# The last key block in 64-row tiles, with its values kept twice beside zeros, and the loading of gated weights alternated with bias additions

## Chip, cores and metric

The kernel runs on one core of a Trainium2 chip. The metric is the device time of one execution in microseconds, and the figure for a kernel is the median of its runs. The engines are named as the profile names them: PE multiplies matrices (PEld is its loading of weights), DVE, ACT and POOL work on elements, and SP issues most of the transfers.

## What is computed

One transformer block on x of 2 x 1024 x 256 with a context of 2 x 154 x 192, all in float32: self-attention, attention to the context, and a gated feed-forward layer, each behind a LayerNorm and with a residual. There are 16 heads of 64.

```python
def _attention(xq, xkv, wq, wk, wv, wo, bo):
    ...
    attn = jnp.einsum('bihd,bjhd->bhij', q, k) * scale
    attn = jax.nn.softmax(attn, axis=-1)
    out = jnp.einsum('bhij,bjhd->bihd', attn, v).reshape(B, S, D_ATTN)
    return out @ wo + bo
h = _layernorm(x, ln1_g, ln1_b)
x = _attention(h, h, sa_wq, sa_wk, sa_wv, sa_wo, sa_bo) + x
h = _layernorm(x, ln2_g, ln2_b)
x = _attention(h, cond_emb, ca_wq, ca_wk, ca_wv, ca_wo, ca_bo) + x
h = _layernorm(x, ln3_g, ln3_b)
p = h @ ff_w1 + ff_b1
a, gate = (p[..., :D_FF], p[..., D_FF:])
h = a * jax.nn.gelu(gate, approximate=False) @ ff_w2 + ff_b2
return h + x
```

## The kernel before

**Three loops of slots.** All work is issued in an order written out by hand. A first loop of 128 slots (`p`) does self-attention, a second of 48 slots (`c`) does the attention to the context, and a third (`k`, counted on as `c = 48 + k` by the helpers of the second) does the feed-forward layer. A unit is one pair of heads of one batch, so there are 16 units in each attention. A unit of self-attention takes eight slots, one of the second attention three (groups of 3, 3 and 2 row tiles of 128 queries). Beside its own work a slot takes pieces from lists: `work` (projections of the next unit), `side` (pieces of a LayerNorm), `outs` (output projections of units that are done), `stores` and `adds` (copies out of PSUM and additions to x, run a little later), and `later` (transfers and bias additions; two entries a slot in the second loop, one in the others).

**A unit of the second attention.** `cross_first(c)` computes scores into two PSUM banks (L654), DVE takes the negated maximum (`neg`, L659), ACT the exponents with their sums (L670), DVE the reciprocals (`rden`, L678), POOL scales (L681). Two slots on, `cross_turn` transposes 32x32 blocks on DVE into a ring of three units (`pT_ca`, L697). The context's 154 keys are padded with zeros to 160, five blocks of 32. `cross_regroup` moves the first four blocks of the ring by transfers (L714, on SP) into `pairs`, a part of the tile `wf`, so that pairs of blocks lie in 64 rows. The fifth block stays in the ring: its rows 32 x a4 to 32 x a4 + 31 hold the keys 128 to 159 for the quarter a4 of the queries.

**Weighing.** `cross_values(ui, a2)` does two of the four quarters, a2 and 2 + a2, seven slots after the unit's first slot for a2 = 0 and eight for a2 = 1. For m = 0 and 1 it takes 64-row tiles from `pairs`; for m = 2 it takes 32-row tiles from the ring. Every float32 matmul of the program appears as two in the profile, so a weighing is 16 matmuls of 64x64 tiles (`poc<-wf,v_ca`) and 8 of 32x64 (`poc<-pT_ca,v_ca`), all on L730. Its sums are copied out by DVE (`o_ca`, L743).

**The values.** `values()` projects values once for two units (L618), in the last slot before the even unit begins: in slot p = 125 of the first loop for unit 0, then at c = 5, 11, 17, 23, 29, 35 and 41. In the next slot ACT copies them (L627, and L628 for the fifth block, 32 rows). Entries put at the head of `later` copy by transfers: L630 mirrors the first blocks into the other 64 rows, and L635 repeats the 32 rows of the fifth block at rows 32, 64 and 96. The tile has the tag `V`, with two buffers that the self-attention's values also use.

**PSUM.** Projections, keys (L606), values and the LayerNorm transposes (`ph_ln`, L227, copied out by ACT on L240) share two banks in turn (`mm_tile`). In the first slot of a unit two q projections stand one behind the other (L299, copied on L308), so the second needs a bank that something else has freed.

**LayerNorms beside.** While the second attention runs, the LN2 of the second batch (slots 9 to 17) and the LN3 of the first batch (around slots 39 to 46) are done in pieces: statistics (L196, L197) and offset (`off_ln`, L212) on DVE, variance and power on POOL (L202, L206), normalizing on ACT (`xn_ln`, L218), transposes on PE, and L240.

**The gated layer's weights.** At c = 5 `hold_gated()` takes a buffer for `wf` and appends 12 transfers of 256 KB to `later`: 8 for w1 (L794) and 4 for w2 (L797). `add_biases("ca", 0)` appends 8 additions of the bias to x on POOL (L261) behind them. Since the copies of values go to the head of the list and take slots 6, 12 and 18, the transfers run in slots 5 and 7 to 11, the additions in 13 to 16.

**Self-attention, as far as it matters here.** A slot p computes two groups of scores (L382), DVE reduces them (L542), ACT takes exponents (L393). Partial maxima and sums are exchanged between rows by transfers (`st<-st`, L403); the slot after joins them (`dd` L411 to L413 on POOL, `ee` L415 on ACT, `zz` and `den` L417 and L419 on POOL, `rd` L489 on DVE) and scales on POOL (L493). DVE transposes the groups of two slots ago (L507), and `weigh` multiplies with the values (`po`, L429, 64x64 tiles).

Of the kernel before, what the change touches and what calls it, by code (L numbers as in the profile page):

```python
# [8 lines left out]
F32 = mybir.dt.float32  # L9
# [4 lines left out]
P = 128  # L14
# [4 lines left out]
def tile_transformer_block(ctx: ExitStack, tc: tile.TileContext, a: dict, out: bass.AP):  # L19
    nc = tc.nc  # L20
# [6 lines left out]
    DF = w["ff_w2"].shape[0]  # L27
    DH = 64
# [5 lines left out]
    NC = D // P  # L34
    CC = DC // 2
    KP = T // 2
    KB = 32
    NB = -(-T // KB)
    VC = 2 * P
    HB = 512  # L40
    QG = 2 * KB
    TP = NB * KB
    NM = P // QG
# [4 lines left out]
    NF = DF // P  # L48
# [10 lines left out]
    pt_ = ctx.enter_context(tc.tile_pool(name="pt", bufs=2))  # L59
# [5 lines left out]
    def mm_tile(name):  # L65
        return ps_m.tile([P, HB], F32, tag="mm", name=name)
# [23 lines left out]
    row_of, r = {}, 0  # L90
# [9 lines left out]
    for n in names[:2]:  # L100
        k = w[n].shape[0] // P
        nc.scalar.dma_start(
            out=cols[:, row_of[n]:row_of[n] + k], in_=w[n].rearrange("(r p) -> p r", p=P)
# [3 lines left out]
    def load_bias(n):  # L107
        bias[n] = one.tile([P, D], F32, tag="bias", name=n)
        nc.sync.dma_start(out=bias[n], in_=w[n].partition_broadcast(P))
# [26 lines left out]
    for n in names[2:]:  # L136
        k = w[n].shape[0] // P
        nc.sync.dma_start(
            out=rows[row_of[n] - n_cols:row_of[n] - n_cols + k, :],
            in_=w[n].rearrange("(r p) -> r p", p=P),  # L140
# [34 lines left out]
    hT, vs, qk, oT = {}, {}, {}, {}  # L175
# [79 lines left out]
    def add_biases(kind, b):  # L255

        bo = {"sa": "sa_bo", "ca": "ca_bo", "ff": "ff_b2"}[kind]

        def add(t):
            xs = xt[b, t // GT][:, t % GT, :]  # L260
            nc.gpsimd.tensor_tensor(xs, xs, bias[bo], ALU.add)  # L261

        later.extend(lambda t=t: add(t) for t in range(NT))
        if b == B - 1 and kind != "ff":
            later.append(lambda: load_bias({"sa": "ca_bo", "ca": "ff_b2"}[kind]))
# [174 lines left out]
    later = []  # L440
# [151 lines left out]
    def cross_pieces(b, pr):  # L592

        t = {}

        def q(n):
            if n == 0:
                t["q"] = p2.tile([P, S], F32, tag="QT", name=f"q_ca{b}_{pr}")
                t["k"] = p2.tile([P, S], F32, tag="KT", name=f"k_ca{b}_{pr}")
                qk["ca", b, pr] = (t["q"], t["k"])  # L600
            return project_half(t["q"], f"q_ca{b}_{pr}", wsl["ca", pr, "q"], hT["ca", b], n, scale)

        def keys():
            pk = mm_tile(f"pk_ca{b}_{pr}")
            for c in range(2):
                nc.tensor.matmul(  # L606
                    pk[:, :T], lhsT=wsl["ca", pr, "k"][:, c, :],
                    rhs=ctxT[:, c, b * TP:b * TP + T], start=(c == 0), stop=(c == 1),
                )
            return lambda: nc.scalar.copy(t["k"][:, :T], pk[:, :T])  # L610

        def values():

            v = vs["ca", b, pr // 2] = pt_.tile([P, NM + 1, VC], F32, tag="V", name=f"v_ca{b}_{pr}")
            pv = mm_tile(f"pv_ca{b}_{pr}")
            for n, rows_ in ((0, P), (1, KB)):
                for c in range(2):
                    nc.tensor.matmul(  # L618
                        pv[:rows_, n * VC:(n + 1) * VC],
                        lhsT=ctxT[:, c, b * TP + n * P:b * TP + n * P + rows_],  # L620
                        rhs=wsl["ca", pr, "v"][:, c, :], start=(c == 0), stop=(c == 1),
                    )

            def store():
                for n in range(NM):
                    own = slice(n * QG, (n + 1) * QG)
                    nc.scalar.copy(v[own, n, :], pv[own, :VC])  # L627
                nc.scalar.copy(v[:KB, NM, :], pv[:KB, VC:])  # L628
                later.insert(0, lambda: [
                    nc.sync.dma_start(  # L630
                        out=v[(1 - n) * QG:(2 - n) * QG, n, :], in_=v[n * QG:(n + 1) * QG, n, :])
                    for n in range(NM)
                ])
                later.insert(1, lambda: [
                    nc.sync.dma_start(out=v[a4 * KB:(a4 + 1) * KB, NM, :], in_=v[:KB, NM, :])  # L635
                    for a4 in range(1, P // KB)
                ])

            return store

        return [lambda: q(0), lambda: q(1), keys] + ([values] if pr % 2 == 0 else [])
# [74 lines left out]

    def cross_values(ui, a2):

        b, pr = units[ui]
        v, v0 = vs["ca", b, pr // 2], pr % 2 * P  # L720
        if a2 == 0 and pr % HP == 0:
            oT["ca", b, pr // HP] = pt_.tile([P, HP, S], F32, tag="oT", name=f"o_ca{b}_{pr}")
        quarters = (a2, 2 + a2)
        po = {a4: sum_tile(f"poc_{ui}_{a4}") for a4 in quarters}
        for m in range(NM + 1):
            for a4 in quarters:
                r0, n = (a4 // 2 * QG, QG) if m < NM else (a4 * KB, KB)
                r = slice(r0, r0 + n)
                for j in range(2):
                    nc.tensor.matmul(  # L730
                        po[a4][j * DH:(j + 1) * DH, :NT * KB],
                        lhsT=v[r, m, v0 + j * DH:v0 + (j + 1) * DH],
                        rhs=pTc["pairs"][r, a2, m, j] if m < NM else
                        pTc["ring"][r, ui % 3, NB - 1, j, :],
                        start=(m == 0), stop=(m == NM),
                        tile_position=(r0, j * DH),
                    )
        dst = oT["ca", b, pr // HP][:, pr % HP, :].rearrange(
            "p (t a q) -> p t a q", a=P // KB, q=KB)

        def store():
            for a4 in quarters:
                nc.vector.tensor_copy(  # L743
                    dst[:, :, a4, :], po[a4][:, :NT * KB].rearrange("p (t q) -> p t q", q=KB)
                )

        return store
# [36 lines left out]
    def hold_gated():  # L784

        wf = pt_.tile([P, 2 * NK, QH // 2], F32, tag="pT", name="wf").rearrange("p a b -> p (a b)")
        n1, n2 = NC * 2 * DF, NF * D
        w1 = wf[:, :n1].rearrange("p (c f) -> p c f", c=NC)
        w2 = wf[:, n1:n1 + n2].rearrange("p (f d) -> p f d", f=NF)
        pTc["pairs"] = wf[:, n1 + n2:n1 + n2 + 2 * NM * 2 * NT * KB].rearrange(  # L790
            "p (a m j q) -> p a m j q", a=2, m=NM, j=2)

        def part1(c, f):
            nc.sync.dma_start(out=w1[:, c, f:f + HB], in_=w["ff_w1"][c * P:(c + 1) * P, f:f + HB])  # L794

        def part2(f):
            nc.sync.dma_start(  # L797
                out=w2[:, f:f + 2, :],
                in_=w["ff_w2"][f * P:(f + 2) * P, :].rearrange("(f p) d -> p f d", p=P),
            )  # L800

        later.extend(
            lambda c=c, f=f: part1(c, f) for c in range(NC) for f in range(0, 2 * DF, HB))
        later.extend(lambda f=f: part2(f) for f in range(0, NF, 2))
        return w1, w2

    def gate_slot(k):

# [54 lines left out]
    with tc.manual_schedule():  # L863
# [68 lines left out]
        for c in range(CA):  # L932
            if c == 0:
                pTc["ring"] = pt_.tile(
                    [P, 2 * NK, QH // 2], F32, tag="pT", name="pT_ca"
                ).rearrange("p a b -> p (a b)")[:, :3 * 2 * NB * NT * KB].rearrange(
                    "p (u n j q) -> p u n j q", u=3, n=NB, j=2)
            if c == 1:
                out_pieces("sa", B - 1, 0, range(NT - 2, NT))
            if c == SH + 1:  # L940
                out_pieces("sa", B - 1, 1, range(NT))
                outs.append(lambda: load_out("ca"))
            if c == SH + 1:
                w1, w2 = hold_gated()
                add_biases("ca", 0)
            if c % len(CG) == 0:
                cross_beside(c // len(CG))
            if c % len(CG) == len(CG) - 1:
                work.extend(held)
                held.clear()  # L950
            flush(adds)
            then = cross_first(c)
            flush(stores)
            flush(lates)
            lates.append(then())
            if c <= SH:
                self_drain(SA + c)
            cross_regroup(c)
            cross_drain(c)
            cross_weigh(c)  # L960
            flush(stores)
            run_work(2, 1, n_sum=2 * (SH < c < 2 * NPAIR and c % len(CG) == 0))
            if SH - LAG < c <= SH:
                run(lambda: self_values(2 * NU - 1, c - SH + LAG - 1))
            for _ in range(min(2, len(later))):
                later.pop(0)()

        for k in range(FF):
            c = CA + k
# [56 lines left out]
```

## Time and profile before

| what | value |
|---|---|
| median of 3 runs | 1164.09 us (1163.5 to 1164.53) |
| the profiled execution | 1164.57 us, of which span 1162.8 |
| PE busy | 1139.2 us, 98% of the span |
| PEld, DVE, ACT, POOL busy | 58%, 71%, 55%, 58% |
| granted PE clock | full throughout |
| moved by DMA | 51.21 MB, mean 44 GB/s |
| L730 matmuls, 64x64 tiles | 512, median 376 ns |
| L730 matmuls, 32x64 tiles | 256, median 400 ns |

The span is cut from the profiled execution alone; the rest of its time lies around the span. [...]neighbours overlap, so what a sequence of matmuls costs is read from the starts: from the first matmul of one group to the first of the next.

### The profile page before, as it was taken

What the parts mean: (1) busy time and instruction counts of PE and PEld (TensorE: products, weight loads), DVE (VectorE), ACT (ScalarE), POOL (GpSimd) and SP (SyncE); (2) the same over time, 40 slices, a digit from 0 to 9 for tenths busy, and PEclk for the clock granted to TensorE, in tenths of its full rate; (3) what the DMA queues carried; (4) which work ended last, traced back from release to release, by engine and by line L of the source; (5) the groups of instructions that cost most, each with busy time, mean ns of one, the idle gap of its engine ahead of it and who ended that gap; (6) DMA issues with size and microseconds to landing.
All of it is one profiled execution on the core that took longest, in us unless ns stands there. A gap on an engine that the chain in (4) does not pass through costs nothing.

```text
span 1162.8 us, 31708 instructions
## 1 busy us (share of the span) xinstructions
PE 1139.2 (98%) x11931; PEld 672.2 (58%) x11931; DVE 829.5 (71%) x1170; ACT 644.5 (55%) x2055; POOL 669.2 (58%) x1556
## 2 busy tenths in 40 slices
PE   8999999999999999999999999999999999999998
PEld 6434444545545545545545544565566567888887
DVE  4888998898889898888999899557555664232222
ACT  5656676666666666656666766538655572041111
POOL 1777777887877777777777777528644453030000
PEclk9999999999999999999999999999999999999999
DMA  2311011101101101101111010167444433000000
GB/s 79 96 44 34 12 26 34 21 17 34 21 21 35 21 17 30 24 18 21 26 25 21 17 29 7 50 159 180 114 105 99 99 83 68 6 14 10 19 10 18
DMA packets 87250, 51.21 MB, mean 44 GB/s; under 512 B 30830, under 2 KB 77882, under 8 KB 87098
## 3 DMA queue, kind: packets, MB, share of 16 engines
q1 hardware_dynamic: 83738, 46.44, 17.5%
q10 hardware_dynamic: 3360, 2.76, 0.8%
q8 instruction: 94, 1.54, 0.5%
q14 instruction: 58, 0.48, 0.1%
HBM read 19.52 MB, written 2.10 MB: 19 GB/s over the span
## 4 chain that ended last, share of the span: by engine, by line
PE 79%; ACT 8%; DVE 4%; POOL 3%; DMA 3%; issue 2%; SPq 1%; DVEq 0%; ACTq 0%; POOLq 0%
PE po L429 15%; PE s L382 15%; PE pa L818 10%; ACT p L393 6%; PE py_ca L360 5%; PE pf L841 5%; PE py_sa L360 5%; PE pq_ca L299 4%; PE poc L730 4%; PE pk_sa L299 4%; PE pq_sa L299 4%; PE pv_sa L315 3%; PE sc L654 3%; DVE st L542 2%; DMA st<-st 2%
## 5 line engine op out<-in xcount | busy, mean ns | idle before, releaser
L393 ACT ACTIVATE p<-s,st 128x512 f32<-128x512 f32 x512 | 345.2, 686 | 219.3 <-DVE st L542 209.8
L493 POOL TENSOR_SCALAR p<-p,rd,ee 128x512 f32<-128x512 f32 x512 | 387.6, 773 | 44.2 <-DVE rd L489 43.2
L542 DVE TENSOR_REDUCE st<-s 128x2 f32<-128x1024 f32 x256 | 301.2, 1218 | 43.8 <-PE s L382 35.4
L507 DVE STREAM_TRANSPOSE pT<-p 128x1024 f32<-128x1024 f32 x256 | 302.3, 1218 | 1.3 <-POOL p L493 1.3
L382 PE MATMUL s<-k_sa,q_sa 64*32 64x512 f32 x4096 | 253.9, 596 | 14.0 <-ACT p L393 12.7
L429 PE MATMUL po<-pT,v_sa 64*64 64x256 f32 x4096 | 235.8, 379 | 0.0
L429 PEld LDWEIGHTS po<-pT,v_sa 64*64 64x64 f32 x4096 | 150.4, 133 | 109.2 <-issue 40.3
L681 POOL TENSOR_SCALAR p<-p,rden 128x154 f32<-128x154 f32 x256 | 97.4, 402 | 111.5 <-DVE rden L678 111.0
L670 ACT ACTIVATE p<-sc,neg 128x154 f32<-128x154 f32 x256 | 96.0, 394 | 87.0 <-DVE rden L678 82.7
L382 PEld LDWEIGHTS s<-k_sa,q_sa 64*32 64x32 f32 x4096 | 60.0, 105 | 144.8 <-ACT p L393 57.1
L818 PE MATMUL pa<-hT_ln,wf 128*128 128x256 f32 x512 | 121.0, 379 | 0.0
L827 DVE SCALAR_TENSOR_TENSOR u<-pa,cols,gate 128x256 f32<-128x256 f32 x64 | 30.9, 483 | 124.2 <-ACT gate L824 124.2
L824 ACT ACTIVATE gate<-pa,cols 128x256 f32<-128x256 f32 x64 | 30.3, 474 | 152.1 <-PE pa L818 152.1
L818 PEld LDWEIGHTS pa<-hT_ln,wf 128*128 128x128 f32 x512 | 96.8, 190 | 13.7 <-issue 0.8
L393 ACT ACTIVATION_READ_ACCUMULATOR p<-s,st 128x1 f32 x512 | 103.8, 203 | 0.0
L659 DVE TENSOR_REDUCE neg<-sc 128x6 f32<-128x924 f32 (+1 forms) x48 | 48.5, 1011 | 48.9 <-PE sc L654 48.9
L417 POOL TENSOR_TENSOR zz<-ee,st 128x8 f32<-128x8 f32 x128 | 26.0, 203 | 78.2 <-ACT ee L415 78.2
L315 PEld LDWEIGHTS pv_sa<-sa_wv,hT_ln 128*128 128x128 f32 x512 | 59.1, 192 | 15.8 <-issue 14.1
L841 PE MATMUL pf<-wf,u 128*128 128x256 f32 x256 | 65.0, 379 | 0.2 <-DVE u L827 0.2
L315 PE MATMUL pv_sa<-sa_wv,hT_ln 128*128 128x128 f32 x512 | 62.2, 278 | 0.0
L360 PE MATMUL py_ca<-ca_wo,o_ca 128*128 128x256 f32 x256 | 60.8, 384 | 0.3 <-ACT hT_ln L240 0.3
L299 PE MATMUL pk_sa<-hT_ln,sa_wk 128*128 128x512 f32 (+1 forms) x132 | 60.6, 596 | 0.3 <-ACT q_sa L308 0.3
(73 smaller groups left out, 1228.8 us busy)
## 6 DMA issues: line engine op xcount, KB each, us to landing
wf<-pT_ca SPq DMA_DIRECT2D x128, 128.0 KB, 2.4
st<-st SPq DMA_DIRECT2D x512, 1.0 KB, 1.7
v_sa<-v_sa SPq DMA_DIRECT2D x64, 128.0 KB, 2.5
wf<-in_L_xattn_ff_w_dram SPq DMA_DIRECT2D x12, 256.0 KB, 4.8
sa_wq<-in_L_xattn_sa_wq_dram SPq DMA_DIRECT2D x16, 128.0 KB, 3.2
sa_wk<-in_L_xattn_sa_wk_dram SPq DMA_DIRECT2D x16, 128.0 KB, 2.4
sa_wv<-in_L_xattn_sa_wv_dram SPq DMA_DIRECT2D x16, 128.0 KB, 2.6
ca_wq<-in_L_xattn_ca_wq_dram SPq DMA_DIRECT2D x16, 128.0 KB, 2.4
```

What stands on the lines that cost most here:

```text
L299: nc.tensor.matmul(pq[:, own], lhsT=wt[:, c, :], rhs=h[:, c, n * HB + own.start:n * HB + own.stop], start=(c == 0), stop=(c == NC - 1),)
L315: nc.tensor.matmul(pv[:, i * P:(i + 1) * P], lhsT=h[:, c, (n * GT + i) * P:(n * GT + i + 1) * P], rhs=wt[:, c, :], start=(c == 0), stop=(c ...
L360: nc.tensor.matmul(py[:, :D], lhsT=o[:, i, t * P:(t + 1) * P], rhs=wo[kind][:, half * HP + i, :], start=(i == 0), stop=(i == HP - 1),)
L382: nc.tensor.matmul(sc[a4 * KB:(a4 + 1) * KB, j, :], lhsT=q[r, c:c + KB], rhs=k[r, h * HB:(h + 1) * HB], start=True, stop=True, tile_positi ...
L393: nc.scalar.activation(pr[:, j, :], sc[:, j, :], AF.Exp, bias=st[:, 0, 0, i, j:j + 1], accum_out=st[:, 0, 1, i, j:j + 1],)
L429: nc.tensor.matmul(po[a2][j * DH:(j + 1) * DH, :QH // 2], lhsT=v[r, t, e, j * DH:(j + 1) * DH], rhs=pT[r, j * NK + n, :], start=(t == 0 an ...
L493: nc.gpsimd.tensor_scalar(pr[:, j, :], pr[:, j, :], rd[:, c:c + 1], ee[:, 0, c:c + 1], op0=ALU.mult, op1=ALU.mult,)
L507: nc.vector.transpose(halves[h][:, :, c:c + KB], groups.pop(0).rearrange("p j (n k) -> p (j n) k", k=KB))
L542: nc.vector.tensor_reduce(st[:, 0, 0, i, :], sc[i], AX.X, ALU.max, negate=True)
L681: nc.gpsimd.tensor_scalar(pr_[:, j, i, :T], pr_[:, j, i, :T], rden[:, j, i:i + 1], 1.0, op0=ALU.mult, op1=ALU.mult,)
L818: nc.tensor.matmul(pa[:, half, :TF * P], lhsT=w1[:, c, half * DF + f * P:half * DF + (f + 1) * P], rhs=h[:, c, t0 * P:(t0 + TF) * P], star ...
L841: nc.tensor.matmul(sums[blk][i][:, :D], lhsT=sums[blk, "u"][:, f, i * P:(i + 1) * P], rhs=w2[:, f, :], start=(f == 0), stop=(f == NF - 1),)
```

## The change

The tile of values has a fourth block beside the two pairs and the fifth. Both places for the fifth block are set to zero by DVE. The values of the fifth block for the even quarters (rows 0 and 64) go into one place, those for the odd quarters (rows 32 and 96) into the other. A weighing of the even quarters (a2 = 0) takes the first place, one of the odd quarters the second, in 64-row tiles: the 32 rows that belong to the other quarter meet zeros. The number of matmuls and of transfers is the same.

The 12 transfers of gated weights are no longer appended in one run. They alternate, entry by entry, with what else stands in `later`, which is the 8 additions, filled up with entries that do nothing. With two entries a slot this gives one transfer and one addition a slot: transfers in slots 5, 7 to 11, 13 to 17 and 19, additions in 5, 7 to 11, 13 and 14.

```diff
         def values():
-            v = vs["ca", b, pr // 2] = pt_.tile([P, NM + 1, VC], F32, tag="V", name=f"v_ca{b}_{pr}")
+            v = vs["ca", b, pr // 2] = pt_.tile([P, NM + 2, VC], F32, tag="V", name=f"v_ca{b}_{pr}")
+            nc.vector.memset(v[:, NM:, :], 0.0)
             pv = mm_tile(f"pv_ca{b}_{pr}")
...
                 later.insert(1, lambda: [
-                    nc.sync.dma_start(out=v[a4 * KB:(a4 + 1) * KB, NM, :], in_=v[:KB, NM, :])
+                    nc.sync.dma_start(out=v[a4 * KB:(a4 + 1) * KB, NM + a4 % 2, :], in_=v[:KB, NM, :])
                     for a4 in range(1, P // KB)
                 ])
...
     def cross_values(ui, a2):
...
             for a4 in quarters:
-                r0, n = (a4 // 2 * QG, QG) if m < NM else (a4 * KB, KB)
-                r = slice(r0, r0 + n)
+                r0 = a4 // 2 * QG
+                r = slice(r0, r0 + QG)
                 for j in range(2):
                     nc.tensor.matmul(
                         po[a4][j * DH:(j + 1) * DH, :NT * KB],
-                        lhsT=v[r, m, v0 + j * DH:v0 + (j + 1) * DH],
+                        lhsT=v[r, m + a2 * (m == NM), v0 + j * DH:v0 + (j + 1) * DH],
                         rhs=pTc["pairs"][r, a2, m, j] if m < NM else
                         pTc["ring"][r, ui % 3, NB - 1, j, :],
...
     def hold_gated():
...
-        later.extend(
-            lambda c=c, f=f: part1(c, f) for c in range(NC) for f in range(0, 2 * DF, HB))
-        later.extend(lambda f=f: part2(f) for f in range(0, NF, 2))
-        return w1, w2
+        parts = [lambda c=c, f=f: part1(c, f) for c in range(NC) for f in range(0, 2 * DF, HB)]
+        parts.extend(lambda f=f: part2(f) for f in range(0, NF, 2))
+        return w1, w2, parts
...
             if c == SH + 1:
-                w1, w2 = hold_gated()
+                w1, w2, parts = hold_gated()
                 add_biases("ca", 0)
+                others = later[:] + [lambda: None] * (len(parts) - len(later))
+                later[:] = [fn for pair in zip(parts, others) for fn in pair] + others[len(parts):]
```

## The prediction

> **What bounds the kernel now.** I read the page first (shares by engine, chain of waits), then windows over the part that the change touches, then the timelines of PE, DVE and ACT there. PE is busy 98% of the span and carries 79% of the chain. The cross stage is the stretch from about 725 to 988 us:
>
> ```profile
> 751.00:795.00 44.00, 43.99 (x296) 27.98 (x292) 25.89 (x61) 21.60 (x97) 18.34 (x54) 1.00 0.72 181
> 795.00:803.00 8.00, 7.20 (x78) 4.11 (x76) 5.61 (x15) 6.57 (x26) 4.84 (x12) 1.00 0.73 149
> 803.00:925.00 122.00, 122.00 (x916) 72.70 (x912) 71.07 (x154) 71.46 (x319) 64.53 (x180) 1.00 0.46 109
> 925.00:960.00 35.00, 34.24 (x289) 21.99 (x292) 23.47 (x61) 26.04 (x103) 18.55 (x53) 1.00 0.35 77
> ```
>
> After the window come its length, then busy us of PE, PEld, DVE, ACT, POOL, then clock, DMA share and GB/s. PE is full but for 0.8 us in 795 to 803 and 0.76 us in 925 to 960; DVE and ACT are near 60%. So PE time saved here shortens the program, except where one of those gaps, or one hidden just behind PE, takes it. A full PE is not an efficient one; starts in PE's timeline show what an order costs:
>
> ```profile
> 742.09 3.68 PE L429 MATMUL po<-pT,v_sa 64*64 64x256 f32 x64
> 745.71 1.06 PE L654 MATMUL sc<-k_ca,q_ca 64*128 64x154 f32 x12
> ...
> 809.28 1.09 PE L730 MATMUL poc<-wf,v_ca 64*64 64x256 f32 x16
> 810.31 0.66 PE L730 MATMUL poc<-pT_ca,v_ca 32*64 32x256 f32 x8
> 810.90 0.79 PE L606 MATMUL pk_ca<-ctxT,ca_wk 96*128 96x154 f32 x4
> ```
>
> From start to next start, 64 matmuls of 64-row tiles take 3.62 us and 16 take 1.03. The difference is 2.59 us for 48, so 0.054 us each [...], and what is left, 1.03 - 16 x 0.054 = 0.17 us, is paid once per run of matmuls in one tiling. The 8 matmuls of 32-row tiles take 0.59 us: 0.43 for the work at the same rate, 0.16 for a second change of tiling.
>
> [...] here the rows of L730 have 376 ns (64 rows) and 400 ns (32 rows) as medians, so doubling the rows with zeros is free. [...] no DVE memset is in this trace.
>
> **The change, part by part.**
>
> *64-row tiles.* All 24 matmuls of a weighing are now alike: 24 x 0.054 + 0.17 = 1.47 us against 1.62. That is 0.15 us saved, 32 times (16 units, two halves): at most 4.9 us. No matmul is added.
>
> *Memset.* Eight instructions (one per two units) on DVE, 128x512 f32. DVE's transpose of 1024 elements takes 1218 ns and of 480, 638: about 1.07 ns per element and 0.13 fixed, hence 0.67 us at most as a row, some 0.57 behind other work, where the fixed part overlaps (two 1024-element reductions take 2.36 us, not 2.44). [...] Sum 4.6 us, but only the exposed ones count. It waits for the V buffer's previous readers; at c=11, the tightest reuse, those are the weighing whose copies out stand just ahead on DVE, so no new wait arises. Behind it are the next maximum reduction, LN statistics, and ACT's copy L628.
>
> First, in the self stage (slot p=125), there is no slack:
>
> ```profile
> 712.62 2.36 DVE L507 STREAM_TRANSPOSE pT<-p 128x1024 f32<-128x1024 f32 x2
> 715.08 0.18 DVE L489 RECIPROCAL rd<-den 128x4 f32<-128x4 f32 x1
> 715.39 2.35 DVE L542 TENSOR_REDUCE st<-s 128x2 f32<-128x1024 f32 x2
> ```
>
> The memset falls between L489 and L542. From there the chain of waits runs reduction, exponents, ee, den, rd, then the last exchange (landing at 730.0), then ACT's ee and q copies, for which PE waits 1.46 us at 731.71. Nothing in it gives: +0.57 us.
>
> Second, at c=12 (values issued in slot 11), where ACT holds PE up already:
>
> ```profile
> 791.40 1.09 ACT L218 ACTIVATE xn_ln<-x,off_ln,rstd_ln 128x256 f32<-128x256 f32 x2 [1.29 <-DVE off_ln L212]
> 792.40 0.74 ACT L627 COPY v_ca<-pv_ca 64x256 f32<-64x256 f32 x2
> 793.16 0.36 ACT L628 COPY v_ca<-pv_ca 32x256 f32<-32x256 f32 x1
> ```
>
> DVE runs without a gap from the reduction at 784.00 to off_ln at 791.24; the memset comes in front of the last statistics. ACT's xn, then L627/L628, follow off_ln, and the second q projection needs the PSUM bank that L628 frees (its pair of projections takes 3.98 us, elsewhere 3.70). So +0.57 again, and the 0.15 of the two weighings of slots 10 and 11 is lost in the same wait. The other six have cover: at c=23, 29 and 35 ACT waits 1.1 us for PE's values; at c=17 the copies start 0.4 us after the memset would end; at c=5 and 41 the projection that needs the bank starts 3.1 and 2.3 us after L628. Without that cover each would cost up to 0.57.
>
> *Gated weights one a slot.* The 12 transfers of 256 KB (L794, L797) and 8 additions (L261) stay the same in number. Transfers now run from c=5 to 19 rather than to 11; additions move from c=13-16, two a slot, to c=5-14. SP's order keeps each regrouping (L714) ahead of its slot's transfer, so a transfer can only slow the landings. This concerns one wait:
>
> ```profile
> 799.25 0.79 PE L654 MATMUL sc<-k_ca,q_ca 64*128 64x154 f32 x8
> 800.27 0.65 PE L730 MATMUL poc<-wf,v_ca 64*64 64x256 f32 x4 [0.22 <-DMA wf<-pT_ca]
> 801.49 1.08 PE L730 MATMUL poc<-wf,v_ca 64*64 64x256 f32 x12 [0.57 <-DMA wf<-pT_ca]
> 802.50 0.66 PE L730 MATMUL poc<-pT_ca,v_ca 32*64 32x256 f32 x8
> ```
>
> By starts it costs more than the 0.8 us of gap: scores of eight take 0.72 us and sixteen tiles 1.03, so 802.50 would have been 801.00: 1.5 us. Its regrouping landed 5.45 us after issue (median 2.4), with 1 MB of ca_wo and four gated pieces around it and the DMA share at 0.99 in 790 to 800. Two pieces less is 0.5 MB, some 2.5 us at the 200 GB/s there, so the wait goes. What is late next is ACT, with LN2 of the second batch: from 800.45 it runs without a gap, and its copies L240 (805.05 to about 806.05) free the bank for the second q projection of c=15, which started at 806.48. Of 1.5 us, and 0.3 from weighings 13 and 14, only 0.43 is kept. The additions lie on POOL, 7 to 10 us busy in 10 there but with nothing behind them that PE waits for: nothing. In the other direction, transfers at c=13-19 raise a DMA share of 0.3 to 0.63 by about 0.17 (1.5 MB in 37 us): nothing, as 0.75 at 770 to 780 made no wait.
>
> *LN3, 925 to 960.* From the scores at 941.25 a chain through DVE and ACT sets the transpose at 951.81; the two weighings inside (942.24, 945.73) save nothing.
>
> **Sum**: memsets +1.14; weighings of c=7, 8, 16, 17: -0.61; the DMA wait -0.43; units 4 to 15, 24 weighings less two: -3.37. Together -3.3 us. The profiled execution took 1164.57 us (span 1162.8 and 1.8 around it), which gives 1161.3; it lies 0.5 above the median of the runs, 1164.09, so I forecast 1160.8.
>
> **The rivals.**
> 1. *More is kept.* ACT's tight places give way, since bias additions have left POOL there and transfers land earlier[...]: up to -4.9 - 1.5 + 0.6 = -5.8 us, 1158.3 from the median. Against it: the ACT rows have no gap that POOL or DMA ends.
> 2. *Less is kept.* Memsets push two or three more slots where ACT is near PE (c=17, 41, 43), 0.6 each, and the DMA wait stays: -3.3 + 0.4 + 1.5 = -1.4 us, 1162.7; with memsets at 0.7, 1163.0.
> 3. [...] 32-row tiles cost as much as they do for another reason that persists: savings zero, memsets +1.1, wait -0.4: +0.7, 1164.8, no change. Against it: the new form is that of po, whose rate is measured.
> 4. *Slower: the spread transfers hit the regroupings at c=13-19.* Each weighing that waits loses what c=14 lost, 1.5 us. There are five in those slots (13, 14, 16, 17, 19): +7.5 in all, less 3.3: +4.2, 1168.3. It decides from four waits of 1.5 us (6 - 3.3 = +2.7). Against: two transfers a slot in c=7-11 caused one such wait only.
>
> **How the numbers follow.** A measurement of this kernel can tell about 0.2%, 2.3 us, from no change. Forecast case 0.60 (its own range -2.2 to -4.4), rival 1 0.18, rival 2 0.12, rival 3 0.05, rival 4 0.05. Faster: 0.18 and 0.56 of the forecast case, with a little of rival 2: 0.76. Same: rivals 2 and 3 and the edge: 0.19. Slower: 0.05. The range 1158.3 to 1163.0 leaves out rivals 3 and 4 and about a tenth shared by the ends.
>
> **What would show it.** Right: no 32*64 rows in L730, 24 matmuls in about 1.47 us start to start; eight DVE MEMSET rows of 0.55 to 0.67 us; no PE wait for wf<-pT_ca near 800; the second q projection of c=12 about 0.6 us later against the scores of c=10, and that of c=15 waiting for L240. Wrong: a weighing still at 1.6 us, or L730 waiting for DMA in c=13-19.

## The result, and the profile after

The changed kernel takes 1161.35 us (median of 13 runs, 1159.91 to 1162.85) against 1164.09 for the kernel before (13 runs too, 1163.18 to 1166.85). The ratio is 0.9973, with a 95% interval from 0.9964 to 0.9981: faster by 0.27%, or by 2.2 to 4.2 us. The forecast was 1160.8 within 1158.3 to 1163.0. The profiled execution took 1161.83 us, of which span 1160.1.

L730 has become L737, L628 is L632, L714 is L718. PE's timeline of the changed kernel, the same places as before:

```profile
743.24 3.68 PE L429 MATMUL po<-pT,v_sa 64*64 64x256 f32 x64
...
810.29 1.09 PE L737 MATMUL poc<-wf,v_ca 64*64 64x256 f32 x16
811.20 0.61 PE L737 MATMUL poc<-pT_ca,v_ca 64*64 64x256 f32 x8
811.74 0.79 PE L606 MATMUL pk_ca<-ctxT,ca_wk 96*128 96x154 f32 x4
```

All 24 matmuls are 64*64 now. From the first start (810.29) to the next group's (811.74) a weighing takes 1.45 us, where it took 1.62; the medians over the weighings without a wait are 1.46 and 1.61. The first sixteen take 0.91, not 1.03, because no change of tiling stands behind them; 1.47 had been forecast for all 24.

The place where DVE has no slack in the self stage, and ACT's place at c=12 with PE's second q projection behind it:

```profile
716.23 0.18 DVE L489 RECIPROCAL rd<-den 128x4 f32<-128x4 f32 x1
716.46 0.48 DVE L618 MEMSET v_ca<- 128x512 f32 x1
716.86 2.29 DVE L542 TENSOR_REDUCE st<-s 128x2 f32<-128x1024 f32 x2
```

```profile
792.73 1.09 ACT L218 ACTIVATE xn_ln<-x,off_ln,rstd_ln 128x256 f32<-128x256 f32 x2 [1.80 <-DVE off_ln L212]
793.73 0.74 ACT L631 COPY v_ca<-pv_ca 64x256 f32<-64x256 f32 x2
794.50 0.36 ACT L632 COPY v_ca<-pv_ca 32x256 f32<-32x256 f32 x1
```

```profile
792.09 1.98 PE L299 MATMUL pq_ca<-hT_ln,ca_wq 128*128 128x512 f32 x4
794.91 1.98 PE L299 MATMUL pq_ca<-hT_ln,ca_wq 128*128 128x512 f32 x4 [0.84 <-ACT v_ca L632]
```

In brackets stands how long the engine was idle and what ended it. ACT's wait for off_ln grew from 1.29 to 1.80 us, and PE now stands 0.84 us in front of the second projection.

The stretch where a weighing had waited 0.22 and 0.57 us for its regrouping:

```profile
801.15 1.09 PE L737 MATMUL poc<-wf,v_ca 64*64 64x256 f32 x16
802.07 0.61 PE L737 MATMUL poc<-pT_ca,v_ca 64*64 64x256 f32 x8
803.10 0.66 PE L227 MATMUL ph_ln<-ident,xn_ln 128*128 128x128 f32 x4 [0.42 <-ACT k_ca L610]
803.68 1.06 PE L658 MATMUL sc<-k_ca,q_ca 64*128 64x154 f32 x12
804.67 1.98 PE L299 MATMUL pq_ca<-hT_ln,ca_wq 128*128 128x512 f32 x4
807.39 1.98 PE L299 MATMUL pq_ca<-hT_ln,ca_wq 128*128 128x512 f32 x4 [0.73 <-ACT hT_ln L240]
```

The transfer wait is gone, and right behind it PE waits for ACT: 0.42 us for L610, and at 807.39 0.73 us for L240. The waits of PE from 752 to 1000, longest first (us in total, times, longest):

```profile
PE ph_ln L227 <- ACT k_ca L610: 0.8, 2, 0.4
PE pq_ca L299 <- ACT v_ca L632: 0.8, 1, 0.8
PE pq_ca L299 <- ACT hT_ln L240: 0.7, 1, 0.7
PE ph_ln L227 <- ACT hT_ln L240: 0.4, 1, 0.4
PE py_ca L360 <- ACT hT_ln L240: 0.3, 1, 0.3
```

No line of it is a transfer: the one transfer a slot from c=13 to 19 delayed no weighing.

**A ruler.** The self stage does not take the same time in every execution, so I compare from the first scores of slot c=3 to the end of the span, and in pieces between the first scores of slots. All numbers are us from the profiles of one execution each.

| kernel | c=3 starts at | c=3 to end | 3-10 | 10-13 | 13-16 | 16-18 | 18-43 | 43-46 |
|---|---|---|---|---|---|---|---|---|
| before | 737.47 | 425.33 | 45.43 | 12.59 | 12.81 | 8.72 | 124.23 | 12.88 |
| changed | 738.62 | 421.48 | 45.10 | 13.11 | 12.47 | 8.49 | 121.69 | 12.87 |
| tiles_only | 736.68 | 421.42 | 45.11 | 13.10 | 12.47 | 8.48 | 121.68 | 12.87 |
| order_only | 738.52 | 424.98 | 45.42 | 12.63 | 12.48 | 8.72 | 124.23 | 12.87 |
| switch_more | 736.16 | 429.24 | 45.75 | 12.64 | 12.46 | 9.06 | 126.80 | 12.87 |
| memset_twice | 736.07 | 422.03 | 45.10 | 13.76 | 12.47 | 8.48 | 121.68 | 12.87 |
| memset_last | 737.23 | 420.97 | 45.11 | 12.65 | 12.47 | 8.49 | 121.68 | 12.87 |
| copies_shared | 736.71 | 423.59 | 45.11 | 13.09 | 12.25 | 8.49 | 122.36 | 13.97 |
| last_shared | 737.26 | 424.84 | 45.11 | 12.65 | 12.24 | 8.49 | 122.37 | 15.65 |
| shared_old_order | 737.30 | 423.60 | 45.10 | 12.60 | 12.74 | 8.48 | 122.37 | 13.97 |
| last_ln2 | 736.51 | 421.39 | 45.10 | 12.63 | 12.22 | 8.48 | 122.37 | 12.87 |
| last_ln2_old | 738.00 | 421.50 | 45.10 | 12.59 | 12.45 | 8.48 | 122.36 | 12.87 |

The span is read to 0.1 us, so the totals to the end are good to 0.05. Pieces that an edit doesn't touch repeat to 0.02 us, except where a weighing waits for a transfer: shared_old_order and last_ln2_old are the same program up to the LN3 of the first batch, and 13-16 took 12.74 us in one and 12.45 in the other. The change is worth -3.85 us on this ruler; the medians of the runs give -2.74.

### The profile page after: what moved, and what is told of

The parts are those of the page before. It is cut to its first block, busy times and chain, and to the rows that moved or that the text cites. A ratio compares the mean times of both kernels' runs of the same rounds, so it can differ in the third digit from the quotient of the medians.

```text
span 1160.1 us, 31720 instructions
## 1 busy us (share of the span) xinstructions
PE 1134.3 (98%) x11931; PEld 675.6 (58%) x11931; DVE 833.0 (72%) x1178; ACT 643.4 (55%) x2055; POOL 665.9 (57%) x1556
## 4 chain that ended last, share of the span: by engine, by line
PE 80%; ACT 7%; DVE 4%; POOL 3%; DMA 2%; issue 2%; SPq 1%; DVEq 0%; ACTq 0%; POOLq 0%
PE po L429 17%; PE s L382 15%; PE pa L824 10%; ACT p L393 5%; PE py_ca L360 5%; PE pf L847 5%; PE py_sa L360 5%; PE pq_ca L299 4%; PE poc L737 4%; PE pk_sa L299 4%; PE pq_sa L299 3%; PE pv_sa L315 3%; PE sc L658 3%; DVE st L542 2%; DMA st<-st 2%
## 5 line engine op out<-in xcount | busy, mean ns | idle before, releaser
L542 DVE TENSOR_REDUCE st<-s 128x2 f32<-128x1024 f32 x256 | 301.3, 1218 | 45.8 <-PE s L382 38.5
L382 PE MATMUL s<-k_sa,q_sa 64*32 64x512 f32 x4096 | 253.9, 596 | 14.2 <-ACT p L393 13.1
L382 PEld LDWEIGHTS s<-k_sa,q_sa 64*32 64x32 f32 x4096 | 59.9, 105 | 145.1 <-ACT p L393 53.8
L299 PE MATMUL pq_ca<-hT_ln,ca_wq 128*128 128x512 f32 x128 | 60.0, 608 | 1.6 <-ACT v_ca L632 0.8
```

What stands on the lines that cost most here:

```text
L299: nc.tensor.matmul(pq[:, own], lhsT=wt[:, c, :], rhs=h[:, c, n * HB + own.start:n * HB + own.stop], start=(c == 0), stop=(c == NC - 1),)
L382: nc.tensor.matmul(sc[a4 * KB:(a4 + 1) * KB, j, :], lhsT=q[r, c:c + KB], rhs=k[r, h * HB:(h + 1) * HB], start=True, stop=True, tile_positi ...
L542: nc.vector.tensor_reduce(st[:, 0, 0, i, :], sc[i], AX.X, ALU.max, negate=True)
```

## The experiments

**tiles_only**: the 64-row tiles and memsets, with the gated weights in the old order.

```diff
-                later[:] = [fn for pair in zip(parts, others) for fn in pair] + others[len(parts):]
+        later.extend(
+            lambda c=c, f=f: part1(c, f) for c in range(NC) for f in range(0, 2 * DF, HB))
+        later.extend(lambda f=f: part2(f) for f in range(0, NF, 2))
```

> The 64-row tiles with their memsets, the gated weights in the old order. Compared from the first scores of the second attention to the end of the span (438.2 us before, 434.4 after), so that the self stage is left out. Theory (LN2's copies on ACT take what the removed transfer wait gives): within 0.4 us of the changed kernel there, 434.4 to 434.8, since the second q projection of c=15 then waits for L240 anyway; the second q projection of c=12 waits about 0.8 us for L632. Rival (the order of the transfers is worth its 1.5 us): about 435.9, with a weighing at c=14 that waits for wf<-pT_ca. In the timed runs: theory ratio to the kernel before 0.9973 as the change has, rival 0.9985.

Measured: 421.42 from c=3 (434.27 from the first scores of the second attention, against 434.38); runs 1160.15 us, ratio 0.9967 (0.9955 to 0.998). In PE's timeline both waits stand behind each other:

```profile
800.05 0.86 PE L737 MATMUL poc<-wf,v_ca 64*64 64x256 f32 x10 [0.18 <-DMA wf<-pT_ca]
...
805.45 1.13 PE L299 MATMUL pq_ca<-hT_ln,ca_wq 128*128 128x512 f32 x2 [0.40 <-ACT hT_ln L240]
```

The transfer wait is there, while the 0.42 us for L610 is gone and the wait for L240 is 0.40 us instead of 0.73: what the first takes these two give back. Slots 13 to 16 take 12.47 us either way. The alternating order adds nothing beside the tiles.

**order_only**: the alternating alone, with 32-row tiles and no memsets.

```diff
+                later[:] = [fn for pair in zip(parts, others) for fn in pair] + others[len(parts):]
```

> The alternating of transfers and additions alone, 32-row tiles kept, no memsets. Theory: the wait of the weighing at c=14 is gone, but of its 1.5 us only 0.4 stays, so 437.8 us from the first scores of the second attention to the end (438.2 before), and a wait of the second q projection of c=15 for L240 appears. Rival: the 1.5 us stays, 436.7. A further rival, transfers at c=13 to 19 that hit regroupings: over 438.2, with waits for wf<-pT_ca in that stretch.

Measured: 424.98 from c=3, 0.35 less than before, nearly all of it in 13-16 (12.48 for 12.81: slot 14 is 1.32 us shorter, slot 15 0.99 longer). From the first scores of the second attention it is 438.20, level with before, since PE's keys of c=1 waited 1.8 us instead of 1.5, ahead of anything that the order touches. In runs 1163.78 us, ratio 0.9996 (0.9988 to 1.0005). No weighing waits for a transfer, and the wait moved on:

```profile
807.13 1.98 PE L299 MATMUL pq_ca<-hT_ln,ca_wq 128*128 128x512 f32 x4 [0.73 <-ACT hT_ln L240]
```

Neither rival holds: the 1.5 us did not stay, and the spread transfers hit nothing.

**switch_more**: the kernel before, with one change of tiling more in each weighing.

```diff
-        for m in range(NM + 1):
+        for m in (0, NM, 1):
...
-                        start=(m == 0), stop=(m == NM),
+                        start=(m == 0), stop=(m == 1),
```

> The kernel before with the 32-row block weighed between the two 64-row blocks, so each weighing has one more change of tiling (64, 32, 64) and the same matmuls, with nothing else changed. Theory (a change of tiling costs about 0.16 us): each weighing takes 1.78 us instead of 1.62 from its first start to the next group's, 32 times 0.16 is +5.1 us, less what waits hide in slots 10, 11, 13, 14, 43 and 44, so +4 to +5 us from the first scores of the second attention to the end. Rival (32-row tiles are themselves slow, no cost of changing): 0 us, 1.62 us each.

Measured: 441.83 from the first scores of the second attention, +3.6; from c=3 429.24, +3.91; runs 1167.63 us, ratio 1.0039 (1.0026 to 1.0053). PE's timeline:

```profile
811.66 0.66 PE L730 MATMUL poc<-wf,v_ca 64*64 64x256 f32 x8
812.25 0.66 PE L730 MATMUL poc<-pT_ca,v_ca 32*64 32x256 f32 x8
812.84 0.66 PE L730 MATMUL poc<-wf,v_ca 64*64 64x256 f32 x8
813.44 2.11 PE L618 MATMUL pv_ca<-ca_wv,ctxT 96*128 96x256 f32 x8
```

Each block of eight takes 0.59 to 0.60 us, 64-row ones too, and the weighing 1.78. The 0.16 us belongs to the change of tiling and not to the 32-row tile. Nor is it the change of operand from `pairs` to the ring: the changed kernel still goes over to the ring for its last eight matmuls, in the same tiling, and pays nothing (its 24 matmuls take 1.46 us, which is 24 x 0.054 and one change of 0.16). The total misses the lower bound by 0.4: 0.3 lie ahead of c=3, where PE's keys of c=1 waited 1.2 us instead of 1.5, and 0.35 were not in my sum, since with PE later the transfer wait of c=14 vanished (13-16: 12.46).

**memset_twice**: every memset of the changed kernel issued twice.

```diff
             nc.vector.memset(v[:, NM:, :], 0.0)
+            nc.vector.memset(v[:, NM:, :], 0.0)
```

> The changed kernel with every memset of zeros issued twice, so eight more of 485 ns on DVE. Theory (exposed only where DVE's chain reaches PE): the second q projection of c=12 waits 0.5 us longer (1.3 us instead of 0.84), and the first one, in slot p=125, whose 0.3 us on DVE did not reach PE, now adds 0 to 0.5 before PE's keys of c=1; the other six nothing. From the first scores of the second attention to the end +0.5 to +1.0 us (434.9 to 435.4). Rival (DVE matters at every memset): +3.9 us. Rival (none is exposed): 0.

Measured: 434.75, and from c=3 422.03, +0.55 over the change, all of it in 10-13 (+0.65; the totals are good to 0.05 each); runs 1162.27 us, ratio 0.9991 (0.9981 to 1.0).

```profile
793.01 1.98 PE L299 MATMUL pq_ca<-hT_ln,ca_wq 128*128 128x512 f32 x4 [1.49 <-ACT v_ca L633]
```

That is 0.65 and not the 0.5 expected, because the second memset waits for the first, whose tile it writes too, and starts 0.66 us after it (788.58 to 789.24):

```profile
789.24 0.48 DVE L619 MEMSET v_ca<- 128x512 f32 x1 [0.17 <-DVE v_ca L618]
```

The other pieces are unchanged, so of the seven memsets of the second loop one is exposed. For the first memset, in slot 125, I count from the second group of scores of that slot, in the nine profiles that kept their clock there:

| memsets in slot 125 | profiles | PE's first scores of the second attention | last exchange issued | PE's keys of c=1 |
|---|---|---|---|---|
| none | before, order_only, switch_more | 15.2 | 17.0 | 22.31, 22.63, 22.00 |
| one | changed, tiles_only, memset_last, last_shared, last_ln2_old | 15.2 | 17.3 | 22.30, 22.26, 22.01, 22.16, 21.98 |
| two | memset_twice | 15.6 | 17.9 | 22.60 |

So one memset delays the exchange by 0.3 us and PE's scores by nothing. What it adds at the keys of c=1 is less than the scatter of 0.6 us there.

**memset_last**: the memset behind the slot's other pieces on DVE.

```diff
-            nc.vector.memset(v[:, NM:, :], 0.0)
+            ends.append(lambda: nc.vector.memset(v[:, NM:, :], 0.0))
...
             run_work(2, 1, n_sum=2 * (SH < c < 2 * NPAIR and c % len(CG) == 0))
+            flush(ends)
```

> The changed kernel with each memset issued on DVE at the end of its slot, behind the LayerNorm statistics, instead of ahead of them. Theory (at c=12 the memset delays off_ln, ACT's normalizing and L632): the wait of the second q projection of c=12 falls from 0.84 us to about 0.4, and from the scores of c=3 to the end of the span 421.0 us (421.5 in the changed kernel, 425.3 before). Rival (the memset delays ACT's copy L632 wherever it stands, since L632 has to follow it): 421.5, the wait stays 0.84.

Measured: 420.97 from c=3, -0.51 against the change, 0.46 of it in 10-13; runs 1160.27 us, ratio 0.9958 (0.9946 to 0.997), the lowest ratio of all, though its interval overlaps that of the change.

```profile
793.08 1.98 PE L299 MATMUL pq_ca<-hT_ln,ca_wq 128*128 128x512 f32 x4 [0.39 <-ACT v_ca L632]
```

So the memset had reached PE through off_ln and ACT's normalizing, not through the copy that must follow it, and the 0.46 us is what it had cost there.

**copies_shared**: half of the LayerNorm copies on DVE.

```diff
-                    if first and (c == 0 or t % 4 == 0):
+                    if first and (c == 0 or t % 4 == 0) or not narrow(kind, b) and c == 0:
```

> The changed kernel with half of the copies of the transposed LayerNorm (c == 0 of L240) on DVE instead of ACT, for LN2 of the second batch and for both LN3. Theory (ACT, in order, is what is late next at c=14, 15 and around c=43 to 46): the waits of PE for L610 and L240 there, 0.42 and 0.73 us in slots 14 and 15 and 1.1 us in slots 44 and 45, mostly go, and c=13 to 16 takes 11.4 to 11.8 us instead of 12.47; from the scores of c=3 to the end 419.5 to 420.5. Rival (DVE's chain is as late as ACT's there): no less than 421.3, with off_ln later by the copies.

Measured: 423.59 from c=3, 2.1 more than the change; runs 1163.19 us, ratio 0.9985 (0.9979 to 0.9991). The theory failed as a remedy: 13-16 gained 0.22 only, and 18-43, 43-46 and the rest lost 0.67, 1.10 and 0.6. At 950.06 PE waits for L240, and ACT's timeline shows L240 itself idle until DVE:

```profile
950.06 1.99 PE L360 MATMUL py_ca<-ca_wo,o_ca 128*128 128x256 f32 x8 [1.74 <-ACT hT_ln L240]
```

```profile
949.44 0.56 ACT L240 ACTIVATE hT_ln<-ph_ln,cols 128x256 f32<-128x256 f32 x1 [2.17 <-DVE rden L682]
```

DVE's half (948.81) stands behind the maximum of the next slot's scores, which waits for PE. ACT's half (949.44) starts only after DVE's is done (948.81 and 0.53), and so the copies that were to relieve PE wait for PE's later work. That ACT's half waits for DVE's because both write one tile is my reading; no run tests it.

**last_shared** joins the two edits above.

> Both: memsets at the end of their slots, and half of the copies on DVE. Theory: the two add up, 419.0 to 420.0 us from the scores of c=3 to the end, that is 1.5 to 2.5 less than the changed kernel; about 0.9955 of the kernel before in the timed runs. Rival: what one gives the other takes, 420.5 or more.

Measured: 424.84 from c=3, 5 us over what was expected of the sum; runs 1163.85 us, ratio 0.9989 (0.998 to 0.9999). The 0.46 of memset_last is there (10-13: 12.65) and so is the loss, 1.7 us larger in 43-46: behind the gap PE's granted clock fell to 0.58 and 0.57 in two windows (the column ahead of the last two), and the eight matmuls there took 3.61 us instead of 1.92:

```profile
948.00:950.00 2.00, 0.42 (x4) 0.18 (x2) 2.00 (x4) 0.45 (x1) 0.36 (x1) 1.00 0.11 23
950.00:952.00 2.00, 1.84 (x5) 1.48 (x6) 0.80 (x3) 2.00 (x12) 1.23 (x5) 0.58 0.00 0
952.00:954.00 2.00, 2.00 (x7) 1.17 (x7) 0.12 (x1) 1.31 (x4) 0.00 (x0) 0.57 0.00 0
```

**shared_old_order** is last_shared with the gated weights in the old order.

> The same as last_shared, but with the gated weights in the old order, two transfers a slot and the additions behind them. Theory (the order of transfers is worth nothing only while ACT is late right behind the wait it removes): now that ACT is relieved the wait of the weighing at c=14 for wf<-pT_ca counts, so from the scores of c=3 to the end 0.5 to 1.5 us more than last_shared. Rival (the order is worth nothing in any case): equal to last_shared within 0.2 us.

Measured: 423.60 from c=3; runs 1163.66 us, ratio 0.9993 (0.9984 to 1.0002). The totals can't be compared as they are, since PE's clock was granted in full behind the gap in this execution (1.00 in the windows from 944 to 962, where last_shared fell to 0.50). Without 43-46 they are 409.63 against 409.19. In 13-16 it takes 12.74 against 12.24, the 0.5 us expected.

**last_ln2** and **last_ln2_old**: the copies shared for LN2 of the second batch alone, with each order.

```diff
-                    if first and (c == 0 or t % 4 == 0) or not narrow(kind, b) and c == 0:
+                    if first and (c == 0 or t % 4 == 0) or kind == "ca" and b == B - 1 and c == 0:
```

> memset_last with half of the copies on DVE for LN2 of the second batch alone, and LN3 as in the change. Theory (the 2.3 us that copies_shared lost came from LN3, where DVE's half stands behind a maximum that waits for PE; LN2's part gained 0.22): from the scores of c=3 to the end 420.7 to 420.8 us, c=13 to 16 in 12.24, no wait of PE over 1 us after c=3. Rival (the copies on DVE cost elsewhere too): over 421.0.

> The same with the gated weights in the old order. Theory (the removed transfer wait is worth what ACT leaves of it): c=13 to 16 in 12.7 instead of 12.24, so 421.2 to 421.3 us from the scores of c=3 to the end, 0.5 more than last_ln2. Rival (the order is worth nothing in any case): equal to last_ln2 within 0.1.

Measured: 421.39 and 421.50 from c=3; runs 1161.03 and 1160.72 us, ratios 0.9971 (0.9959 to 0.9982) and 0.9967 (0.9954 to 0.9979). The first expectation was wrong: the 0.67 in 18-43 stays, so it had come from LN2's copies and not from LN3's. All of it lies in slot 18, where PE did not wait in the change:

```profile
818.33 1.98 PE L299 MATMUL pq_ca<-hT_ln,ca_wq 128*128 128x512 f32 x4 [0.42 <-ACT hT_ln L240]
```

LN3's two pieces are as in the change again. The second was half right: the old order costs 0.23 us in 13-16 (12.45 against 12.22), where it had cost 0.50 in the same program before. How long that weighing waits for its transfer differs from one execution to the next, so these two figures are a range and not two effects. The order is worth what ACT leaves of it: 0.0 in the change, 0.2 to 0.5 with the copies shared, 0.33 without the tiles; in the medians of the runs none of these three can be told from nothing.

## Why the prediction was right

By its own steps, against the table (predicted, then measured):

| step | predicted | measured |
|---|---|---|
| a weighing | 1.47, saves 0.15 | 1.46, saves 0.16 (medians) |
| c=7, 8 (3-10) | -0.31 | -0.33 |
| memset at c=12, weighings 10, 11 lost in it (10-13) | +0.57 | +0.52 |
| transfer wait, weighings 13, 14 (13-16) | -0.43 | -0.34 |
| c=16, 17 (16-18) | -0.30 | -0.23 |
| 16 weighings (18-43) | -2.45 | -2.54 |
| LN3 (43-46) | 0 | -0.01 |
| last 6 weighings (from c=46 to the first sum of the gated layer) | -0.92 | -0.95 |
| from there on | 0 | +0.03 |
| first memset | +0.57 | 0.0, with a scatter of 0.6 |
| rest of the self stage | 0 | +1.15 in the profiles |

- **The cost of a change of tiling** was right in size. switch_more adds one and the change removes one, 0.16 us both times. The runs show the time of a change and not what PE does in it. That the added zero rows are free is shown too: the last eight matmuls have a median of 376 ns, as the first sixteen, where the 32-row ones had 400.
- **The hidden losses** were right. Slots 10 and 11, 13 and 14, 43 and 44 gave nothing of their weighings, and the removed 1.5 us of transfer wait was worth 0.34 because ACT's L610 and L240 were next. One more loss of this kind had not been forecast: the weighing of c=17 gives 0.08 instead of 0.16, because PE's values behind it wait for ACT's L610 (they start 0.63 us after the last eight matmuls, 814.54 to 815.17, where 0.54 is usual). It is there whether the memset stands once, twice or later in its slot.
- **The memset** at c=12 took the path that was named, as memset_last shows, and the other six cost nothing, as memset_twice shows. Its size was too large: DVE's next instruction starts 0.40 us after it (716.46 to 716.86), and it cost 0.46 us at c=12, where 0.57 had been forecast. Its row is 485 ns, where 0.67 was my upper estimate, from DVE's transposes (1218 ns for 1024 elements, 638 for 480). The low end of the range, 1158.3, counts the two exposed memsets at 0.3 us each: that was a guess of mine, which no trace shows.
- **The step that failed** is "Nothing in it gives: +0.57 us" for the first memset. DVE's next reduction came 0.32 us later, not 0.57, since part of the memset filled the 0.13 us in which DVE had been idle before it. The last exchange is issued 0.26 late, and nothing is left of that at PE's keys of c=1 (22.30 us from slot 125 against 22.31): it landed 3.34 us after its issue instead of 3.60. So the exchange gave way, which the prediction had taken as fixed. Why it lands no later is open, and so is whether a part of the 0.3 us is left in an average execution; the five profiles with one memset give 22.14 us on average and the three with none 22.31.
- **The close total is in part luck.** Without the first memset my sum is -3.8, and the ruler shows -3.85. The runs show -2.7 and the forecast was -3.3. The interval of the runs, -2.2 to -4.2, takes in all of them, so the runs can't tell the forecast with the memset exposed from the one without. In the two profiles the part ahead of c=3 was 1.15 us longer in the change, which hides a part of the -3.85. That part isn't the change's doing, as far as these runs tell: the offset is there by 130 us, long before the first instruction that differs, and tiles_only, with the same instructions up to c=5, reaches c=3 1.94 us earlier than the change. What sets it stays open. That the medians fall short of -3.85 for the same reason isn't shown; for tiles_only, whose total from c=3 is within 0.1 us of the change, they give -3.64.

Of the rivals, "less is kept" has no sign in the pieces beyond the 0.08 us at c=17, which is not the memset's doing, and neither the third (32-row tiles that cost as much for another reason) nor the fourth, the slower one, left a trace.

## What to carry to other kernels

A change between 64-row and 32-row tiles cost about 0.16 us each time here, so give a small remainder the tiling of its neighbours, with zeros, where the added rows are free as they were here (medians of 376 ns with the zeros, 400 without). Before counting the gain of a wait that goes, look for the engine that is late right behind it: of 1.5 us, 0.34 were kept. An instruction on an engine that looks idle can cost what stands behind it in that engine's queue: DVE is busy 72% of the span, and the memset ahead of the statistics cost 0.46 us at c=12; the same memset a few instructions later cost next to nothing (12.65 us in 10-13, against 12.59 in the kernel without one).

## What the hardware showed beyond that

- PE's granted clock fell to half (0.50 in the windows of 951 to 953) for 3.4 us, from 950.3 to 953.7, in last_shared, after one gap of 1.75 us, and eight matmuls took 3.61 us instead of 1.92. Behind the same gap there was no drop in copies_shared and shared_old_order (1.00 in every window from 944 to 962). But these two and last_ln2 had such a stretch of 3.4 us earlier, from 709.7, 707.9 and 709.4, in the self stage, behind gaps of 1.51, 2.07 and 1.74 us. Sixteen matmuls of L382 took 1.89 us there to the next start in copies_shared and last_ln2, where last_shared has 1.02, and 32 took 3.52 in shared_old_order, where copies_shared has 1.88 at 704.16 (the clock is again the column ahead of the last two; copies_shared):

```profile
710.00:712.00 2.00, 2.00 (x17) 0.43 (x2) 1.77 (x4) 0.12 (x1) 1.60 (x4) 0.50 0.04 5
```

  In the other eight profiles gaps of 1.3 to 1.8 us brought none (1.84 in switch_more, 1.78 in order_only; the mean granted clock of each of the eight is 1.00). So a slow stretch stood behind a gap in some executions and not in others, and in these twelve the gap's length alone does not decide.
- The twelve profiles, all with the same program up to the first values (slot p=125), have slot c=3 start between 736.1 and 738.6 us. Differences under 2.5 us in one profile are worth reading only from a mark behind which the programs differ.
